# Second attention of a two-layer block: steps of two key blocks, scores in all of PSUM, weighted sums added in SBUF

## The chip, the cores and the metric

The kernel runs on one core of a Trainium2 chip. A core has a matrix engine (TensorE, PE in the profile; its weight loads are PEld), VectorE (DVE), ScalarE (ACT), GpSimd (POOL) and SyncE (SP), which issues most DMAs. Engines run their own instruction queues in order and wait for each other by semaphores. TensorE writes into PSUM, which has 8 banks of 128 x 512 fp32; VectorE and ScalarE read it. Everything here is fp32, and each fp32 matmul of the program appears as two matmuls in the profile, so a "round" below is one pass of 512 columns through the array. The array can be split into tiles that work side by side: four tiles of 64x64, eight of 32x64 (32 rows of contraction, 64 output rows), four of 128x32. The profile writes this shape in each group.

The metric is the time of one execution on the device, in microseconds; less is better.

## The reference

Input x has 16 images of 256 channels and 32x32 = 1024 positions. Layer 0 is an attention with 4 heads of 64; layer 1 is group norm, an attention with 8 heads of 32, group norm and an mlp of 1024 hidden channels.

```
x = res0 @ w_out + b_out + xs                       # layer 0, attention with 4 heads of 64
x = x + attention(group_norm(x, gn1), qkv_w, proj_w, proj_b, phys_bias)   # 8 heads of 32
h = gelu(mlp_w1 @ group_norm(x, gn2) + mlp_b1)
return x + mlp_w2 @ h + mlp_b2
```

In each attention, `softmax(q k^T / sqrt(d)) v`; the bias `phys_bias` is one number per head.

## The kernel before

All 16 images are run by one loop over `b`. For each image: the first attention (`attention_a`), the mlp's hidden half of the image before (`hidden`), the projections of the second attention (`qkv_1`), the second attention (`attention_b`), and then the next image. Work that has no place of its own on TensorE, "pieces", is laid between the steps of the second attention: the projections of its own second channel half (`own`, 7 pieces), the mlp's output half of the image before (`outputs`, 16 half reduces, from `mlp`), and the first attention's projections for the next image (`first`, 12). Image 0 has only its own 7, because it has no predecessor and its `first` pieces ran earlier; image 15 has its own 7 and 8 half reduces, the others being left for the end. Order is written out by hand: the program order of the pieces, and `Later`, a list of functions that run after so many steps (`tick`).

Softmax is done without subtracting a maximum: scores are transposed (keys on partitions), exp goes over them, the weighted sum is a matmul with v, and the sum over keys is made by adding the exps of the 8 key blocks on VectorE (`es`) and one matmul with ones (`den`) per item.

The second attention has 4 items per image: query half t (512 queries) by channel half c (4 heads). One step is one key block of 128 keys: `scores` (L410) makes 4 heads x 128 x 512 scores in four PSUM banks (two `wide` tiles of two banks), ScalarE's exp (L422) reads each wide tile into an `e` tile in SBUF; then `weigh` (L431) multiplies the exps of the step before with v, adding up over all 8 key blocks in one PSUM bank, `acc`. VectorE adds the exps (L448). At the end of an item ScalarE copies `acc` to SBUF (L455), `normalise` makes the denominator (L463) and `denominators` sends it through a small DMA (spread), a reciprocal (L267), a row in DRAM and a broadcast DMA (`rd`) back, after which `scale` (L478) multiplies. When both channel halves of a query half are done, `project` runs the output projection (`j`, through `product`, L246, and L509).

PSUM before: three `wide` tiles of two banks, taken in turn (the one used longest ago is next), and two single banks, used in turn for `acc` and `den`. Scores take two wide tiles a step; a filler takes one. The half reduces of the mlp keep their wide tile (`kept`) over two pieces. With `cols[0]` at 32 the fillers run as 128x32 tiles, the shape of `weigh`, so within a step the array changes shape from 128x32 to 32x64 and back.

`run` calls one step, then `tick`, then the fillers of that step. `gn_g`, from which the own pieces are made, shares its buffer (tag `res`) with the result of query half 0.

Of the kernel before, what the change touches and what calls it, by code (L numbers as in the profile page):

```python
# [8 lines left out]
F32 = mybir.dt.float32  # L9
# [5 lines left out]
P = 128  # L15
# [173 lines left out]
def first_pass(ctx, tc, x, out, k):  # L189
# [10 lines left out]
        tc.tile_pool(name="ps_s", bufs=1, space=bass.MemoryType.PSUM)  # L200
    )
    ps_a = ctx.enter_context(
        tc.tile_pool(name="ps_a", bufs=2, space=bass.MemoryType.PSUM)
    )

    dram = ctx.enter_context(
# [7 lines left out]
    def use(n):  # L214
        order.remove(n)
        order.append(n)
# [4 lines left out]
        use(n)  # L221
        return ps_s.tile([P, 2, TB], F32, tag=f"s{n}", name=name)

    def bank(name):
        return ps_a.tile([P, TB], F32, tag="acc", name=name)


    dsum, isum = (act.tile([P, 4 * TB // P], F32, name=n) for n in ("dsum", "isum"))
# [60 lines left out]
    def attention_a(b, qT, kT, v, project):  # L289
# [24 lines left out]
        def weigh(i, kb, e):  # L314
            t, c = items[i]
            if kb == 0:
                if i % 2:
                    acc = wide(f"acc_{key}_{i}", 2)
                    accs[i] = [acc[:, h, :] for h in range(2)]
                else:  # L320
                    accs[i] = [bank(f"acc_{key}_{i}_{h}") for h in range(2)]
# [12 lines left out]
            if kb == 1:  # L334
                sums[i] = work.tile([P, 2, TB], F32, tag="es", name=f"es_{key}_{i}", bufs=4)
            nc.vector.tensor_add(sums[i], held[i] if kb == 1 else sums[i], e)  # L336
            if kb == SB - 1:
                r = res[:, c, t * TB : (t + 1) * TB]
                one, two = accs.pop(i)
                nc.scalar.copy(r, one)  # L340
                nc.vector.tensor_add(r, r, two)
# [52 lines left out]

    def attention_b(b, qT, kT, v, project):
        key, D = f"b_{b}", D1
        G = P // D
        items = [(t, c) for c in range(CC) for t in range(NT)]  # L400
        units = [(i, kb) for i in range(len(items)) for kb in range(SB)]
        res = {}
        accs, held, sums = {}, {}, {}

        def scores(i, kb):
            t, c = items[i]
            tiles = [wide(f"s_{key}_{i}_{kb}_{n}") for n in range(G // 2)]
            for g in range(G):
                for h in range(0, P, HALF):
                    nc.tensor.matmul(  # L410
                        tiles[g // 2][h : h + HALF, g % 2, :],
                        kT[g * D : (g + 1) * D, c, kb * P + h : kb * P + h + HALF],
                        qT[g * D : (g + 1) * D, c, t * TB : (t + 1) * TB],
                        start=True,
                        stop=True,
                    )
            es = []
            for n, s in enumerate(tiles):
                e = work.tile(
                    [P, 2, TB], F32, tag="e", name=f"e_{key}_{i}_{kb}_{n}", bufs=8  # L420
                )
                nc.scalar.activation(e, s, AF.Exp, scale=float(D) ** -0.5)  # L422
                es.append(e)
            return i, kb, es

        def weigh(i, kb, es):
            t, c = items[i]
            if kb == 0:
                accs[i] = bank(f"acc_{key}_{i}")
            for g in range(G):  # L430
                nc.tensor.matmul(  # L431
                    accs[i][g * D : (g + 1) * D, :],
                    v[:, kb, c * G + g],
                    es[g // 2][:, g % 2, :],
                    start=(kb == 0),
                    stop=(kb == SB - 1),
                )
            if kb == 0:
                held[i] = es
                return  # L440
            if kb == 1:
# [4 lines left out]
            for n, e in enumerate(es):  # L446
                d = sums[i][n]
                nc.vector.tensor_add(d, held[i][n] if kb == 1 else d, e)  # L448
            if kb == SB - 1:
                if t not in res:  # L450
                    res[t] = act.tile(
                        [P, CC, TB], F32, tag="res1" if t else "res", name=f"res_{key}_{t}"
                    )
                r = res[t][:, c, :]
                nc.scalar.copy(r, accs.pop(i))  # L455
                last = i == len(items) - 1
                later.after(1 if last else 2, lambda: normalise(i, r, last))

        def normalise(i, r, last):
            t, c = items[i]  # L460
            den = bank(f"den_{key}_{i}")
            for g in range(G):
                nc.tensor.matmul(  # L463
                    den[g * D : (g + 1) * D, :],
                    k["eones"][:, c * G + g],
                    sums[i][g // 2][:, g % 2, :],
                    start=True,
                    stop=True,
                )
            denominators(  # L470
                f"{key}_{i}", den_copy(f"{key}_{i}", den), TB,
                ((3, 5) if b + 1 < B else (1, 1)) if last else (1, 3),
                lambda full: scale(i, r, last, full),
            )

        def scale(i, r, last, full):
            t, c = items[i]
            tc.keep_in_program_order(nc.vector.tensor_mul(r, r, full))  # L478
            if c == CC - 1:
                wait = (10 if b + 1 < B else 1) if last else 1  # L480
                later.after(wait, lambda: project(t, res[t]))

        cols[0] = D
        pending = None
        for u in units:
            now = scores(*u)
            if pending:
                weigh(*pending)
            pending = now
            yield  # L490
        weigh(*pending)
        yield
        cols[0] = P
# [183 lines left out]


    def mlp(b, xb, hn):
        gs, held, slot = {}, [], []  # L680

        def hidden(t, hc):
            ps = wide(f"m1_{b}_{t}_{hc}")[:, 0, :]
# [9 lines left out]
            nc.scalar.activation(g, ps, AF.Gelu, bias=k["m1b"][:, hc : hc + 1])  # L693
            gs[t, hc] = g


        def reduce(t, co, half, part):
            n = TB // 2
            if part == 0:
                held.append(wide(f"m2_{b}_{t}_{co}_{half}")[:, 0, :n])  # L700
                kept.add(order[-1])
                slot.append(order[-1])
            else:
                use(slot[-1])
                kept.discard(slot.pop())
            ps = held[-1]
            for hc in range(part * HC // 2, (part + 1) * HC // 2):
                product(
                    ps,
                    k["w2"][:, hc, co * P : (co + 1) * P],  # L710
                    gs[t, hc][:, half * n : (half + 1) * n],
                    start=(hc == 0),
                    stop=(hc == HC - 1),
                )
            if part == 0:
                return
# [4 lines left out]
            if half:  # L721
# [5 lines left out]
        return (  # L727
            [lambda t=t, hc=hc: hidden(t, hc) for t in range(NT) for hc in range(HC)],
            [
                lambda t=t, co=co, half=half, part=part: reduce(t, co, half, part)  # L730
                for t in range(NT) for co in range(CC) for half in range(2)
                for part in range(2)
            ],
        )

# [38 lines left out]

    later.after(2, fold_bias)
    hidden, outputs = [], []
    last = NT * CC * SB - 1
    for b in range(B):
        if b + 1 < B:
            xs[b + 1] = load_x(b + 1)  # L780
# [18 lines left out]

        run_pieces(qk[:n] + v[:1])  # L800
        own = [v[1], qk[n], v[2], qk[n + 1], v[3], *qk[n + 2 :]]
        fill = {m: [piece] for m, piece in enumerate(own)}
        rest = outputs + (first if b > 0 else [])
        end = []
        if b == B - 1:

            rest, end = rest[:8], rest[8:]
        for m, piece in enumerate(rest):
            at = len(own) + m * (last + 1 - len(own)) // max(1, len(rest) - 1)
            fill.setdefault(at, []).append(piece)  # L810
        hn = []
        run(
            attention_1(
# [21 lines left out]
    row = bank("ok_row")  # L835
# [290 lines left out]
```

## Time and profile before

| | us |
|---|---|
| runs | 3879.7, 3879.98, 3877.6 (median 3879.7) |
| profiled execution | 3877.58 |
| its span, first to last instruction | 3875.7 |
| TensorE busy | 3846.9 (99%) |
| VectorE busy | 2116.0 (55%) |
| ScalarE busy | 2048.2 (53%) |
| granted TensorE clock, mean | 1.000 |

Group rows read: line, engine, operation, output and inputs, shape, count; busy us in all and mean ns of one; then the idle time of the engine ahead of them and what ended it. Timeline rows read: start (us), length (us), engine, line, operation, and how many instructions were merged. Matmuls are pipelined and overlap, so the length of a TensorE group is more than what it adds; the distance from one group's start to the next is its cost. The first attention, the hidden half and the projections are not touched by the change; the second attention of images 1 to 14 lasts 131.6 us in the image shown in the prediction (1286.9 to 1418.6).

### The profile page before, as it was taken

The numbers are of one execution on the slowest core, as the hardware profiler recorded it, in microseconds if no ns is written. First come the engines' busy times: TensorE is split into PE (matmuls) and PEld (weight loads), VectorE is DVE, ScalarE is ACT, GpSimd is POOL, SyncE is SP. The second block draws the span as 40 slices with busy tenths as digits, with TensorE's granted clock in tenths as the row PEclk, the third lists the DMA queues.
The fourth block names the chain that finished last, engine by engine and source line by source line (L and its number), as shares of the span: only waits on it lengthen the run. The fifth ranks groups of instructions, "written<-read, shape, count | busy, mean of one in ns | idle before, by whom it ended". The sixth has DMA issues, their size and how long they took to land.

```text
span 3875.7 us, 86863 instructions
## 1 busy us (share of the span) xinstructions
PE 3846.9 (99%) x38637; PEld 1435.3 (37%) x38637; DVE 2116.0 (55%) x2569; ACT 2048.2 (53%) x2369; POOL 84.8 (2%) x252
## 2 busy tenths in 40 slices
PE   9999999999999999999999999999999999999999
PEld 3333343333433334333343333333333333333335
DVE  4574545645456455555545556455464555645562
ACT  4654645546455554545545555454554545545461
POOL 1000000000000000000000000000000000000000
PEclk9999999999999999999999999999999999999999
DMA  2000000000000000000000000010000000000000
GB/s 83 12 13 15 27 12 32 13 12 27 12 32 15 10 27 12 32 15 13 29 7 32 15 16 26 7 32 15 16 26 7 32 15 18 24 10 19 14 13 23
DMA packets 62445, 78.54 MB, mean 20 GB/s; under 512 B 35344, under 2 KB 36880, under 8 KB 62064
## 3 DMA queue, kind: packets, MB, share of 16 engines
q1 hardware_dynamic: 57728, 68.72, 5.8%
q8 instruction: 304, 4.98, 0.5%
q10 hardware_dynamic: 3712, 3.80, 0.3%
q14 instruction: 77, 0.63, 0.1%
q0 software_dynamic: 624, 0.41, 0.1%
HBM read 54.54 MB, written 17.56 MB: 19 GB/s over the span
## 4 chain that ended last, share of the span: by engine, by line
PE 92%; DVE 5%; ACT 1%; issue 1%; DMA 0%; POOL 0%; ACTq 0%; SPq 0%; DVEq 0%
PE s_b L410 14%; PE acc_b L431 13%; PE m L685 12%; PE m L246 11%; PE s_a L303 10%; PE acc_a L324 9%; PE qk_b L246 6%; PE qk_a L246 6%; PE v_b L246 3%; PE v_a L246 3%; PE j L246 3%; DVE es_a L336 2%; PE o L246 2%; PE den_b L463 1%; ACT e_a L311 1%
## 5 line engine op out<-in xcount | busy, mean ns | idle before, releaser
L422 ACT ACTIVATE e_b<-s_b 128x1024 f32<-128x1024 f32 x1024 | 994.3, 1023 | 601.4 <-PE s_b L410 596.3
L448 DVE TENSOR_TENSOR es_b<-es_b,e_b 128x1024 f32<-128x1024 f32 x768 | 905.0, 1221 | 436.1 <-ACT e_b L422 436.1
L311 ACT ACTIVATE e_a<-s_a 128x1024 f32<-128x1024 f32 x512 | 520.9, 1024 | 450.6 <-PE s_a L303 437.1
L410 PE MATMUL s_b<-q,k 32*64 32x512 f32 x8192 | 581.4, 613 | 1.2 <-DVE x L509 0.6
L303 PE MATMUL s_a<-q,k 64*64 64x512 f32 x4096 | 562.1, 593 | 2.4 <-DVE x L509 2.4
L324 PE MATMUL acc_a<-e_a,v 64*64 64x512 f32 x4096 | 555.1, 589 | 0.0
L431 PE MATMUL acc_b<-e_b,v 128*32 128x512 f32 x4096 | 546.2, 604 | 0.1
L336 DVE TENSOR_TENSOR es_a<-es_a,e_a 128x1024 f32<-128x1024 f32 x384 | 468.9, 1221 | 111.8 <-ACT e_a L311 107.0
L246 PE MATMUL m<-g,w 128*32 128x256 f32 (+1 forms) x7616 | 482.7, 379 | 0.3 <-DVE mean_h L545 0.3
L685 PE MATMUL m<-gn_h,w 128*128 128x512 f32 x1024 | 458.2, 599 | 3.8 <-DVE mean_g L545 3.8
L246 PEld LDWEIGHTS m<-g,w 128*32 128x32 f32 (+1 forms) x7616 | 279.4, 112 | 253.4 <-issue 101.3
L693 ACT ACTIVATE g<-m,m1b 128x512 f32<-128x512 f32 x256 | 174.2, 687 | 341.4 <-PE m L685 341.2
L448 DVE TENSOR_TENSOR es_b<-e_b,e_b 128x1024 f32<-128x1024 f32 x128 | 151.1, 1222 | 246.8 <-ACT e_b L422 246.8
L324 PEld LDWEIGHTS acc_a<-e_a,v 64*64 64x64 f32 x4096 | 183.2, 133 | 260.9 <-issue 233.0
L685 PEld LDWEIGHTS m<-gn_h,w 128*128 128x128 f32 x1024 | 188.5, 190 | 241.3 <-issue 226.9
L303 PEld LDWEIGHTS s_a<-q,k 64*64 64x64 f32 x4096 | 167.3, 133 | 280.6 <-issue 207.2
L246 PE MATMUL qk_a<-x,wp 128*32 128x512 f32 (+1 forms) x1856 | 244.2, 594 | 7.8 <-DMA wp<-in_L_conv_w_proj_dram 6.0
L410 PEld LDWEIGHTS s_b<-q,k 32*64 32x64 f32 x8192 | 126.0, 129 | 307.8 <-ACT e_b L422 133.6
L246 PE MATMUL qk_b<-gn_g,wq 128*32 128x512 f32 (+1 forms) x1280 | 234.1, 592 | 0.0
L431 PEld LDWEIGHTS acc_b<-e_b,v 128*32 128x32 f32 x4096 | 82.3, 108 | 407.5 <-issue 403.1
L615 DVE TENSOR_TENSOR v<-v_b,eones 128x512 f32<-128x512 f32 x64 | 44.0, 688 | 263.8 <-PE v_b L246 263.8
L246 PEld LDWEIGHTS qk_b<-gn_g,wq 128*32 128x32 f32 (+1 forms) x1280 | 81.9, 126 | 137.4 <-issue 127.8
(111 smaller groups left out, 1986.1 us busy)
## 6 DMA issues: line engine op xcount, KB each, us to landing
x<-in_x_dram SPq DMA_DIRECT2D x32, 512.0 KB, 4.4
rd_a<-row_a SPq DMA_DIRECT2D x64, 256.0 KB, 3.9
rd_b<-row_b SPq DMA_DIRECT2D x256, 64.0 KB, 2.0
out_dram<-x SPq DMA_DIRECT2D x64, 256.0 KB, 2.0
w<-in_L_conv_mlp_w_dram ACTq DMA_DIRECT2D x2, 1024.0 KB, 16.1
sp_b<-d_b SPq DMA_DIRECT2D x64, 8.0 KB
row_b<-inv_b SPq DMA_DIRECT2D x64, 8.0 KB, 1.4
wq<-in_L_conv_qkv_w_dram ACTq DMA_DIRECT2D x1, 768.0 KB, 11.9
```

The lines of the kernel that those rows point to most:

```text
L246: nc.tensor.matmul(o[sl], w[:, sl], r, **flags)
L303: nc.tensor.matmul(s[h : h + HALF, g, :], kT[g * D : (g + 1) * D, c, kb * P + h : kb * P + h + HALF], qT[g * D : (g + 1) * D, c, t * TB : ...
L311: nc.scalar.activation(e, s, AF.Exp, scale=float(D) ** -0.5)
L324: nc.tensor.matmul(accs[i][h][g * D : (g + 1) * D, :], v[h * HALF : (h + 1) * HALF, kb, c * 2 + g], e[h * HALF : (h + 1) * HALF, g, :], st ...
L336: nc.vector.tensor_add(sums[i], held[i] if kb == 1 else sums[i], e)
L410: nc.tensor.matmul(tiles[g // 2][h : h + HALF, g % 2, :], kT[g * D : (g + 1) * D, c, kb * P + h : kb * P + h + HALF], qT[g * D : (g + 1) * ...
L422: nc.scalar.activation(e, s, AF.Exp, scale=float(D) ** -0.5)
L431: nc.tensor.matmul(accs[i][g * D : (g + 1) * D, :], v[:, kb, c * G + g], es[g // 2][:, g % 2, :], start=(kb == 0), stop=(kb == SB - 1),)
L448: nc.vector.tensor_add(d, held[i][n] if kb == 1 else d, e)
L615: nc.vector.tensor_mul(d, ps, v_scale.unsqueeze(1).to_broadcast([P, 2, C // D, D]))
L685: nc.tensor.matmul(ps, k["w1"][:, cc, hc * P : (hc + 1) * P], hn[0][:, cc, t * TB : (t + 1) * TB], start=(cc == 0), stop=(cc == CC - 1),)
L693: nc.scalar.activation(g, ps, AF.Gelu, bias=k["m1b"][:, hc : hc + 1])
```

## The change

One step of the second attention takes two key blocks. Their scores fill all 8 banks: the first block's heads 0 and 1 go into the two single banks (`b0`, `b1`), heads 2 and 3 into a wide tile, the second block's into two wide tiles. The exp of heads 0 and 1 of the first block becomes two instructions of 512 columns. Since no bank is left for an accumulator that lives over an item, `weigh` adds up only the two blocks of a step, in `b0`, and the sum goes to SBUF: by a ScalarE copy in an item's first step, by a VectorE add `res += acc` in the three others. `den` takes `b1`. The exp sums are added in two parts, ahead of and behind `weigh`, in that program order. The items run as (1,0), (0,0), (0,1), (1,1) instead of (0,0), (1,0), (0,1), (1,1) (query half, channel half), so that the partial sums of the first item are not written into the buffer that the own pieces still read. Fillers are laid two old pieces to a step: the mlp's reduces become whole (8 instead of 16 halves, no tile kept over two pieces), `first` goes in groups of two or three, with one piece beside the last own piece and one after the last step. The scale of an item follows one step after its reciprocal (of the new, double steps) instead of three.

```diff
-        tc.tile_pool(name="ps_a", bufs=2, space=bass.MemoryType.PSUM)
+        tc.tile_pool(name="ps_a", bufs=1, space=bass.MemoryType.PSUM)
...
-    def bank(name):
-        return ps_a.tile([P, TB], F32, tag="acc", name=name)
+    def bank(name, n):
+        return ps_a.tile([P, TB], F32, tag=f"b{n}", name=name)
...
     def attention_b(b, qT, kT, v, project):
-        items = [(t, c) for c in range(CC) for t in range(NT)]
-        units = [(i, kb) for i in range(len(items)) for kb in range(SB)]
+        items = [(NT - 1, 0)]
+        items += [(t, 0) for t in range(NT - 1)] + [(t, 1) for t in range(NT)]
+        units = [(i, kb) for i in range(len(items)) for kb in range(0, SB, 2)]
...
-            tiles = [wide(f"s_{key}_{i}_{kb}_{n}") for n in range(G // 2)]
+            for m in range(2):
+                if m == 0:
+                    one, two = (bank(f"s_{key}_{i}_{kb}_{n}", n) for n in range(2))
+                    tiles = [None, wide(f"s_{key}_{i}_{kb}_1")]
+                    outs = [one, two, tiles[1][:, 0, :], tiles[1][:, 1, :]]
+                else:
+                    tiles = [wide(f"s_{key}_{i}_{kb + 1}_{n}") for n in range(2)]
+                    outs = [tiles[g // 2][:, g % 2, :] for g in range(G)]
+                for g in range(G):
+                    for h in range(0, P, HALF):
+                        k0 = (kb + m) * P + h
+                        nc.tensor.matmul(
+                            outs[g][h : h + HALF, :],
...
+                    for to, s in (
+                        [(e, tiles[n])] if tiles[n] is not None
+                        else [(e[:, 0, :], one), (e[:, 1, :], two)]
+                    ):
+                        nc.scalar.activation(to, s, AF.Exp, scale=float(D) ** -0.5)
...
+        def add(i, kb, es, block):
...
+            for n in range(G // 2):
                 d = sums[i][n]
-                nc.vector.tensor_add(d, held[i][n] if kb == 1 else d, e)
+                ins = nc.vector.tensor_add(d, es[n] if kb == 0 else d, es[2 * block + n])
+                if block:
+                    tc.keep_in_program_order(ins)
...
+        def weigh(i, kb, es):
+            t, c = items[i]
+            acc = bank(f"acc_{key}_{i}_{kb}", 0)
+            for m in range(2):
+                for g in range(G):
+                    nc.tensor.matmul(
+                        acc[g * D : (g + 1) * D, :],
+                        v[:, kb + m, c * G + g],
+                        es[2 * m + g // 2][:, g % 2, :],
+                        start=(m == 0),
+                        stop=(m == 1),
+                    )
...
+            if kb == 0:
+                nc.scalar.copy(r, acc)
+            else:
+                nc.vector.tensor_add(r, r, acc)
+            if kb == SB - 2:
+                later.after(1, lambda: normalise(i, r, i == len(items) - 1))
...
-            den = bank(f"den_{key}_{i}")
+            den = bank(f"den_{key}_{i}", 1)
...
-                ((3, 5) if b + 1 < B else (1, 1)) if last else (1, 3),
+                ((3, 5) if b + 1 < B else (1, 1)) if last else (1, 1),
...
             now = scores(*u)
+            add(*now, 0)
             if pending:
                 weigh(*pending)
+            add(*now, 1)
...
-        def reduce(t, co, half, part):
+        def reduce(t, co, half):
-            if part == 0:
-                held.append(wide(f"m2_{b}_{t}_{co}_{half}")[:, 0, :n])
-                kept.add(order[-1])
-                slot.append(order[-1])
-            else:
-                use(slot[-1])
-                kept.discard(slot.pop())
-            for hc in range(part * HC // 2, (part + 1) * HC // 2):
+            ps = wide(f"m2_{b}_{t}_{co}_{half}")[:, 0, :n]
+            for hc in range(HC):
...
-    last = NT * CC * SB - 1
+    last = NT * CC * SB // 2 - 1
...
-        fill = {m: [piece] for m, piece in enumerate(own)}
-        rest = outputs + (first if b > 0 else [])
+        fill = {m: own[2 * m : 2 * m + 2] for m in range((len(own) + 1) // 2)}
+        now, end = outputs, []
+        if b == 0:
+            first = []
         if b == B - 1:
-            rest, end = rest[:8], rest[8:]
-        for m, piece in enumerate(rest):
-            at = len(own) + m * (last + 1 - len(own)) // max(1, len(rest) - 1)
-            fill.setdefault(at, []).append(piece)
+            now, end = outputs[:4], outputs[4:]
+        rest = [[piece] for piece in now]
+        at = len(fill)
+        if first:
+            fill[at - 1] = fill[at - 1] + first[:1]
+            fill[last + 1] = first[-1:]
+            pairs = [first[1:4], first[4:7], first[7:9], first[9:-1]]
+            for m, pair in enumerate(pairs):
+                rest.insert(3 * m + 2, pair)
+        for m, pieces in enumerate(rest):
+            fill[at + m] = pieces
```

More of the change, by code (lines that the diff above doesn't have):

```diff
@@ L320, in weigh @@
                 else:
-                    accs[i] = [bank(f"acc_{key}_{i}_{h}") for h in range(2)]
+                    accs[i] = [bank(f"acc_{key}_{i}_{h}", h) for h in range(2)]
             for h in range(2):
@@ L399, in attention_b @@
         G = P // D
-        items = [(t, c) for c in range(CC) for t in range(NT)]
-        units = [(i, kb) for i in range(len(items)) for kb in range(SB)]
-        res = {}
-        accs, held, sums = {}, {}, {}
+        items = [(NT - 1, 0)]
+        items += [(t, 0) for t in range(NT - 1)] + [(t, 1) for t in range(NT)]
+        units = [(i, kb) for i in range(len(items)) for kb in range(0, SB, 2)]
+        res, sums = {}, {}
         def scores(i, kb):
             t, c = items[i]
-            tiles = [wide(f"s_{key}_{i}_{kb}_{n}") for n in range(G // 2)]
[L408 to L415, printed above, removed]
-                    )
[L417 to L423, printed above, removed]
-            return i, kb, es
@@ L426, in weigh @@
[L426 to L441, printed above, removed]
+            es = []
@@ new lines, in scores @@
+            for m in range(2):
[11 more added lines that the diff above has]
+                            outs[g][h : h + HALF, :],
+                            kT[g * D : (g + 1) * D, c, k0 : k0 + HALF],
+                            qT[g * D : (g + 1) * D, c, t * TB : (t + 1) * TB],
+                            start=True,
+                            stop=True,
+                        )
+                for n in range(G // 2):
+                    e = work.tile(
+                        [P, 2, TB], F32, tag="e", name=f"e_{key}_{i}_{kb + m}_{n}", bufs=8
+                    )
+                    for to, s in (
[3 more added lines that the diff above has]
+                        nc.scalar.activation(to, s, AF.Exp, scale=float(D) ** -0.5)
+                    es.append(e)
@@ L442, in weigh @@
+            return i, kb, es
+        def add(i, kb, es, block):
+            if kb == 0 and block == 0:
                 sums[i] = [
@@ L445, in weigh @@
                 ]
-            for n, e in enumerate(es):
+                return
+            for n in range(G // 2):
                 d = sums[i][n]
[L448 to L452, printed above, removed]
-                    )
[L454 to L457, printed above, removed]
+                ins = nc.vector.tensor_add(d, es[n] if kb == 0 else d, es[2 * block + n])
[12 more added lines that the diff above has]
+                        stop=(m == 1),
+                    )
+            if t not in res:
+                res[t] = act.tile(
+                    [P, CC, TB], F32, tag="res1" if t == NT - 1 else "res",
+                    name=f"res_{key}_{t}",
+                )
+            r = res[t][:, c, :]
+            if kb == 0:
[4 more added lines that the diff above has]
+                later.after(1, lambda: normalise(i, r, i == len(items) - 1))
         def normalise(i, r, last):
             t, c = items[i]
-            den = bank(f"den_{key}_{i}")
+            den = bank(f"den_{key}_{i}", 1)
             for g in range(G):
@@ L679, in mlp @@
     def mlp(b, xb, hn):
-        gs, held, slot = {}, [], []
+        gs = {}
         def hidden(t, hc):
@@ L694, in hidden @@
             gs[t, hc] = g
-        def reduce(t, co, half, part):
+        def reduce(t, co, half):
             n = TB // 2
-            if part == 0:
-                held.append(wide(f"m2_{b}_{t}_{co}_{half}")[:, 0, :n])
-                kept.add(order[-1])
-                slot.append(order[-1])
-            else:
-                use(slot[-1])
-                kept.discard(slot.pop())
-            ps = held[-1]
-            for hc in range(part * HC // 2, (part + 1) * HC // 2):
+            ps = wide(f"m2_{b}_{t}_{co}_{half}")[:, 0, :n]
+            for hc in range(HC):
                 product(
@@ L714, in reduce @@
                 )
-            if part == 0:
-                return
             y = xb[:, co, t * TB + half * n : t * TB + (half + 1) * n]
@@ L729, in mlp @@
             [
-                lambda t=t, co=co, half=half, part=part: reduce(t, co, half, part)
+                lambda t=t, co=co, half=half: reduce(t, co, half)
                 for t in range(NT) for co in range(CC) for half in range(2)
-                for part in range(2)
             ],
@@ L801, in first_pass @@
         own = [v[1], qk[n], v[2], qk[n + 1], v[3], *qk[n + 2 :]]
-        fill = {m: [piece] for m, piece in enumerate(own)}
-        rest = outputs + (first if b > 0 else [])
-        end = []
+        fill = {m: own[2 * m : 2 * m + 2] for m in range((len(own) + 1) // 2)}
+        now, end = outputs, []
+        if b == 0:
+            first = []
         if b == B - 1:
-            rest, end = rest[:8], rest[8:]
-        for m, piece in enumerate(rest):
-            at = len(own) + m * (last + 1 - len(own)) // max(1, len(rest) - 1)
-            fill.setdefault(at, []).append(piece)
+            now, end = outputs[:4], outputs[4:]
[9 more added lines that the diff above has]
+            fill[at + m] = pieces
         hn = []
@@ L834, in first_pass @@
     nc.vector.tensor_mul(both, ok[:, 0:1], ok[:, 1:2])
-    row = bank("ok_row")
+    row = bank("ok_row", 0)
     nc.tensor.transpose(row[0:1, :P], both, k["ident"])
```

## The prediction

> **What bounds the kernel now.** I read the page first (engine shares, chain of waits, groups), then TensorE's waits, then timelines of the second attention in three places: image 5 (filled steps), image 0 (bare steps), and the start of the stage. The page:
>
> ```profile
> PE 3846.9 (99%) x38637; PEld 1435.3 (37%) x38637; DVE 2116.0 (55%) x2569; ACT 2048.2 (53%) x2369; POOL 84.8 (2%) x252
> PE 92%; DVE 5%; ACT 1%; issue 1%; DMA 0%; POOL 0%; ACTq 0%; SPq 0%; DVEq 0%
> L422 ACT ACTIVATE e_b<-s_b 128x1024 f32<-128x1024 f32 x1024 | 994.3, 1023 | 601.4 <-PE s_b L410 596.3
> L448 DVE TENSOR_TENSOR es_b<-es_b,e_b 128x1024 f32<-128x1024 f32 x768 | 905.0, 1221 | 436.1 <-ACT e_b L422 436.1
> ...
> L341 DVE TENSOR_TENSOR res_a<-res_a,acc_a 128x512 f32<-128x512 f32 x64 | 43.8, 684 | 15.1 <-ACT res_a L340 14.6
> L282 ACT COPY d_b<-den_b 128x512 f32<-128x512 f32 x64 | 37.6, 587 | 9.2 <-PE den_b L463 9.1
> ```
>
> TensorE is never free; VectorE and ScalarE idle almost half the time, waiting for it. Only TensorE's own time, or a wait newly put in front of it, can move the end. But its busy time hides what happens between matmul groups. TensorE's timeline in image 5 (start us, length us, group; groups overlap, so starts are compared) shows it:
>
> ```profile
> 1318.04 1.11 PE L410 MATMUL s_b<-q,k 32*64 32x512 f32 x16
> 1319.09 1.07 PE L431 MATMUL acc_b<-e_b,v 128*32 128x512 f32 x8
> 1319.97 1.91 PE L246 MATMUL m<-g,w 128*32 128x256 f32 x32
> 1321.81 1.11 PE L410 MATMUL s_b<-q,k 32*64 32x512 f32 x16
> 1322.86 1.06 PE L431 MATMUL acc_b<-e_b,v 128*32 128x512 f32 x8
> 1323.74 1.04 PE L463 MATMUL den_b<-es_b,eones 128*32 128x512 f32 x8
> 1324.60 1.91 PE L246 MATMUL m<-g,w 128*32 128x256 f32 x32
> ```
>
> A group of two rounds of 512 columns with no change of array shape takes 0.86 us (den, 1323.74 to 1324.60); in the first attention, where every group is 64x64, starts stand 0.86 apart throughout. The scores (32x64) take 1.05 to the next start, 0.19 too much; acc, the first group at 128x32, 0.88, 0.02 too much; the fill of 32 takes 1.84 to the next scores where 32 more of the same cost 1.72 (a fill of 64 runs 3.56), 0.12 too much. So each step pays 0.33 us for going to the 32x64 shape and back. The stage of image 5 (1286.9 to 1418.6, 131.6 us) is its pure work, 120.9, plus 32 x 0.33: nothing else is lost there.
>
> The helpers beside one step (T = 1330.20; the row at 1330.68 is the second score round, from a narrower window), and image 0, where most steps have no fill:
>
> ```profile
> 1330.20 1.11 PE L410 MATMUL s_b<-q,k 32*64 32x512 f32 x16
> ...
> 1330.68 0.63 PE L410 MATMUL s_b<-q,k 32*64 32x512 f32 x8
> ...
> 1331.36 1.94 ACT L422 ACTIVATE e_b<-s_b 128x1024 f32<-128x1024 f32 x2 [1.82 <-PE s_b L410]
> 1332.41 2.36 DVE L448 TENSOR_TENSOR es_b<-es_b,e_b 128x1024 f32<-128x1024 f32 x2 [1.41 <-ACT e_b L422]
> ...
> 162.84 1.11 PE L410 MATMUL s_b<-q,k 32*64 32x512 f32 x16
> 181.23 1.11 PE L410 MATMUL s_b<-q,k 32*64 32x512 f32 x16
> ```
>
> The first exp starts 1.15 after the scores; exps follow each other at 0.92 (two take 1.94, one 1.02), adds at 1.14 (2.36 less 1.22). Image 0 needs 18.39 us for an item of 8 blocks.
>
> **The change, part by part.** Terms are against the profiled execution, 3877.6 us (span 3875.7 and 1.9 around it), which lies 2.1 below the median, 3879.7.
>
> *1. Half the shape changes.* A step now takes two key blocks: four score rounds, four weigh rounds, the fill. 512 steps become 256. In the 14 images with full fill (1 to 14): 16 x 0.33 = 5.33 us each, **-74.6**. Images 0 and 15 are counted below. This holds if the second block's score rounds come at 0.43. Bounds: the first two score rounds start 0.48 apart, and if every round of this shape did, a step would give back 0.10; if the whole 0.19 belonged to each block, 0.19. I take 0, as in the 64x64 rounds, the nearest rows without a change of shape.
>
> *2. A filled step, walked through.* From T: scores to 1.90, weigh 1.90 to 3.64, fill (3.45, two old pieces) to 7.2. ScalarE: the first exp is split into two of 512 columns. No row shows one: half of 1.02 is 0.51, the longest 512 row (Gelu, 0.687) the other end; I take 0.60, near the copy's 0.587, at a pitch of 0.5 (half of 0.92 is 0.46). Starts 1.14, 1.64, then the wide ones 2.14, 3.06, 3.98, end 5.0. The weigh must wait until bank b0 is read: 1.14 + 0.60 + 0.05 (an add starts 0.03 after its exp) = 1.79, before 1.90; at Gelu's length 1.88. Nothing is lost. A filler uses the wide tile read first: free at 3.2, before 3.64. VectorE, in the built order: two adds from 2.27, the new res += acc (0.685 by the L341 row, 192 of them, 132 us in all, beside TensorE) at 4.54, two adds to 7.5, the mlp's output (0.48) from 7.4 to 7.9. Bank b0 is free at 5.2, long before the next scores at 7.2. The filler's tile is free at 7.93, and the next step writes it as its last score tile, at 7.2 + 0.91 = 8.11: 0.17 to spare. So steady steps cost nothing; this narrow margin is the cover to watch. VectorE must next start at 9.5.
>
> A rule weighs against this part. The Trainium skill, "Perfetto Trace Analysis", section "Matmuls", wants independent matmul groups to rotate through PSUM banks, so that evacuation of one overlaps the next. The change does the opposite. Were the emptying of the accumulator exposed in every step, with res += acc ending at 4.55 and TensorE ready at 3.64, it would cost 0.9 x 256 = 230 us, and the sum would come out near 4070. I follow the rows: 3.45 us of fill stand in between.
>
> *3. Division.* The waits of (1,3) steps become (1,1) double ones. Reciprocal at T+6.8; before, the last broadcast landed 5.8 us after the reciprocal (1327.37; issues to 1331.18, 2.0 to land), so T+12.6, 5.4 into the next step; the multiply is due there at 7.4. No wait. But it (0.69, pitch 0.6) stands ahead of the mlp output on VectorE: tile free at 8.53 against 8.11, a stall of 0.43 us. It meets an mlp filler in steps 10 and 14 (step 6 has qk pieces, read by ScalarE): 2 x 0.43 x 14 = **+12.0** (0 to 24).
>
> *4. The first step.* Scores fill all three wide tiles, there is nothing to weigh, and the filler wants the tile whose exp ends at 3.16: TensorE, ready at 1.9, waits 1.26. Before, a third tile was free; only 0.21 was lost (second scores 1.32 instead of 1.11). **+14.7** for 14 images (4 to 18).
>
> *5. Image 0: 12 bare steps.* No fill covers the loop now. With kb = 4 and 6, scores wait for b0: exps 1.14 to 2.24, adds to 4.54, res += acc to 5.2, next scores at 5.25 and 5.75 (behind the multiply). With kb = 2 the accumulator is copied by ScalarE after five exps: 5.0. With kb = 0 b1 waits for the denominator's copy: 5.63. Together 21.6 per item against 18.39. Whole stage: 6.8 (step 0) + 2 x 7.2 + 5.5 + 12 x 5.4 - 2 (covered by the projection) + 3.4 (projection) + 1.7 (last weigh) = 94.7 against 85.9 (130.0 to 215.9): **+8.8** (3 to 14).
>
> *6. Image 15: 8 bare steps.* 6.8 + 14.4 + 5.5 + 4 x 7.2 + 0.4 + 8 x 5.4 - 2 + 3.4 + 1.7 = 102.3 against 102.9 (3686.1 to 3789.0). Before, the half-done reduce held a wide tile, and six scores took 2.00 instead of 1.11 to 1.3; whole reduces end that: **-0.6**.
>
> *7. The rest, at nothing.* Fill, projections, mlp, qkv are the same matmuls; TensorE's order elsewhere is the same. DMAs: no count changes; an output DMA on SP waits for VectorE's mlp add at the end of a step, and what stands behind it on SP, the next spread, is due some 5 us later. POOL keeps its two small adds per item. Item order (query half 1 first) only lets res be written early, because `gn_g` shares half 0's buffer: no time by itself.
>
> Sum: -74.6 + 12.0 + 14.7 + 8.8 - 0.6 = **-39.7**: 3837.9 on the profiled basis, **3840** beside the median.
>
> **Rivals.**
>
> *A. VectorE's end of step becomes the wait (slower).* Place: the last score tile of the 112 steps of images 1 to 14 whose filler ends in the mlp add. For: margin 0.17, and 192 new VectorE reads of PSUM. Against: 56 adds of 1.14 and all else make 83 us of VectorE in a stage of 126, and each step begins with idle VectorE until 2.27. If it runs d late, it costs 112 x (d - 0.17); it decides from d = 0.52, where 39.7 are gone. With d = 0.8: +71, 3910.
>
> *B. The extra belongs to the 32x64 rounds, not to the change of shape (the change doesn't do what it says).* For: 0.48 between the first two. Against: the shortest score matmuls of this shape last 587 ns, no longer than the 64x64 ones (593 in the mean), so nothing but the first round looks stretched. 0.10 x 256: +27, 3867; with 0.19, +49, 3889.
>
> *C. The stalls don't come.* Exps a little shorter or adds more tightly packed take parts 3 and most of 4 away, and image 0 half: -26, 3814.
>
> **How the numbers follow.** My case 0.53 (3822 to 3862); C 0.17; B 0.18 (a third of it over the old time); A 0.12. The range reaches from just under C's time, 3812, to B's upper end, 3888, leaving out A and the last of C, some 2 in 10. A measurement tells 0.2% (7.8 us) from no change: under 3872 faster, 0.80; within, 0.06 (B's middle); over 3887.5, 0.14 (A, and B's upper end).
>
> **What would show it.** Right: steps of 7.2 us in images 1 to 14 with scores of 1.9; TensorE's starts after scores and fill with the same 0.33 per step; the stage near 128 us; bare steps of 5.4 in image 0; about 1.3 us before the first filler, its weight load waiting for an exp. Part 3: score groups stretched by 0.4 after the multiply, released by VectorE's mlp line. Wrong: four score rounds of 2.1 us or more (B); weigh groups waiting for the 512 exps, or score loads waiting for VectorE in most steps (A); or TensorE time moving outside the second attention, which I hold unchanged.

## The result, and where the time went

| | before | after |
|---|---|---|
| median, us | 3879.2 | 3837.0 |
| profiled execution, us | 3877.58 | 3836.97 |
| its span, us | 3875.7 | 3835.1 |

The ratio is 0.9892 [0.9875, 0.9910]; the kernel measured again beside the experiments gave 3836.78 and 0.9899 [0.9883, 0.9916]. Between the profiled executions the change is worth -40.6 us; the sum of the prediction was -39.7.

The page after, engine shares, chain of waits and the group that is new:

```profile
PE 3783.2 (99%) x38637; PEld 1508.9 (39%) x38637; DVE 2214.2 (58%) x2761; ACT 2033.7 (53%) x2625; POOL 86.1 (2%) x252
...
PE 90%; DVE 5%; issue 2%; ACT 2%; DMA 1%; POOL 0%; SPq 0%; ACTq 0%; POOLq 0%; DVEq 0%
...
L477 DVE TENSOR_TENSOR res_b<-res_b,acc_b 128x512 f32<-128x512 f32 x192 | 131.1, 683 | 190.9 <-PE acc_b L461 190.9
```

The same 38637 matmuls take 63.7 us less busy time, yet the end moves by only 40.6. The difference is new waiting on TensorE. TensorE's waits after (who waited, for whom: us in all, times, longest) have three rows that before did not:

```profile
PE v_b L246 <- ACT e_b L437: 19.2, 16, 1.2
...
PE s_b L422 <- DVE res_b L477: 4.9, 8, 0.9
...
PE s_b L422 <- ACT res_b L475: 0.9, 5, 0.2
```

The new `res += acc` costs VectorE 131.1 us in 192 instructions and brings TensorE 4.9 us of listed waits, in 8 places, all in the steps without filler (bare steps) of images 0 and 15. TensorE's timeline of image 5 shows where both signs come from:

```profile
1278.81 1.97 PE L422 MATMUL s_b<-q,k 32*64 32x512 f32 x32
1281.99 1.93 PE L246 MATMUL v_b<-wq,gn_g 128*32 128x256 f32 x32 [1.20 <-ACT e_b L437]
...
1285.57 1.97 PE L422 MATMUL s_b<-q,k 32*64 32x512 f32 x32
...
1315.30 1.97 PE L422 MATMUL s_b<-q,k 32*64 32x512 f32 x32
1317.20 1.92 PE L461 MATMUL acc_b<-e_b,v 128*32 128x512 f32 x16
1318.94 3.64 PE L246 MATMUL m<-g,w 128*32 128x256 f32 x64
1322.51 1.97 PE L422 MATMUL s_b<-q,k 32*64 32x512 f32 x32
...
1392.92 2.40 PE L422 MATMUL s_b<-q,k 32*64 32x512 f32 x32
1395.25 1.92 PE L461 MATMUL acc_b<-e_b,v 128*32 128x512 f32 x16
```

Read starts. A filled step is 1315.30 to 1322.51, 7.21 us: scores 1.90, weigh 1.74, fill 3.57. Four score rounds of 0.43 are 1.72, so they bear 0.18 too much, as two rounds did before (0.19); the weigh bears 0.02 and the fill 0.13. The 0.33 of going to the 32x64 shape and back is the same, paid once for two blocks. Against it stand the 1.20 us ahead of the first filler, and two score groups, behind steps 10 and 14, that take 2.32 to the next start (2.33 in the last rows) instead of 1.90.

By stage, from scores start to scores start: image 1 begins 5.2 us later relative to image 0; each of images 1 to 14 takes 236.72 us in place of 239.92, 3.20 less, -44.8 in all; image 15 with everything behind it is 0.5 shorter, and what is ahead of image 0's stage 0.5 shorter too. That is the whole -40.6. The last 0.5 can't be put down to the change: over the runs of this document image 0's stage begins anywhere from 129.4 to 132.2 us. In image 5 the 3.2 lie inside the second attention (132.67 to 129.48, from its first scores to the next image's first attention); nothing outside it moved.

### The profile page after: what moved, and what is told of

It is laid out like the page before. It is cut to its first block, busy times and chain, and to the rows that moved or that the text cites. A ratio compares the mean times of both kernels' runs of the same rounds, so it can differ in the third digit from the quotient of the medians.

```text
span 3835.1 us, 87391 instructions
## 1 busy us (share of the span) xinstructions
PE 3783.2 (99%) x38637; PEld 1508.9 (39%) x38637; DVE 2214.2 (58%) x2761; ACT 2033.7 (53%) x2625; POOL 86.1 (2%) x252
## 4 chain that ended last, share of the span: by engine, by line
PE 90%; DVE 5%; issue 2%; ACT 2%; DMA 1%; POOL 0%; SPq 0%; ACTq 0%; POOLq 0%; DVEq 0%
PE s_b L422 12%; PE m L709 12%; PE acc_b L461 12%; PE m L246 11%; PE s_a L303 10%; PE acc_a L324 9%; PE qk_b L246 6%; PE qk_a L246 6%; PE v_b L246 3%; PE j L246 3%; PE v_a L246 3%; DVE es_a L336 2%; PE o L246 2%; PE den_b L485 1%; ACT e_a L311 1%
## 5 line engine op out<-in xcount | busy, mean ns | idle before, releaser
L437 ACT ACTIVATE e_b<-s_b 128x1024 f32<-128x1024 f32 (+1 forms) x1280 | 982.7, 864 | 469.4 <-PE s_b L422 469.4
L422 PE MATMUL s_b<-q,k 32*64 32x512 f32 x8192 | 536.3, 601 | 5.8 <-DVE res_b L477 4.9
L461 PE MATMUL acc_b<-e_b,v 128*32 128x512 f32 x4096 | 492.1, 598 | 0.0
L246 PE MATMUL m<-g,w 128*32 128x256 f32 (+1 forms) x7616 | 464.0, 379 | 0.0
L422 PEld LDWEIGHTS s_b<-q,k 32*64 32x64 f32 x8192 | 173.8, 130 | 294.0 <-issue 155.7
L461 PEld LDWEIGHTS acc_b<-e_b,v 128*32 128x32 f32 x4096 | 108.5, 109 | 351.6 <-ACT e_b L437 194.7
L477 DVE TENSOR_TENSOR res_b<-res_b,acc_b 128x512 f32<-128x512 f32 x192 | 131.1, 683 | 190.9 <-PE acc_b L461 190.9
L246 PE MATMUL qk_a<-x,wp 128*32 128x512 f32 (+1 forms) x1856 | 234.1, 594 | 7.2 <-DMA wp<-in_L_conv_w_proj_dram 5.9
```

The lines of the kernel that those rows point to most:

```text
L246: nc.tensor.matmul(o[sl], w[:, sl], r, **flags)
L422: nc.tensor.matmul(outs[g][h : h + HALF, :], kT[g * D : (g + 1) * D, c, k0 : k0 + HALF], qT[g * D : (g + 1) * D, c, t * TB : (t + 1) * TB] ...
L437: nc.scalar.activation(to, s, AF.Exp, scale=float(D) ** -0.5)
L461: nc.tensor.matmul(acc[g * D : (g + 1) * D, :], v[:, kb + m, c * G + g], es[2 * m + g // 2][:, g % 2, :], start=(m == 0), stop=(m == 1),)
L477: nc.vector.tensor_add(r, r, acc)
```

## The experiments

The theory is the prediction's: half of the shape changes go, and waits in three places are paid for that. The rivals are B (the 0.19 belongs to the score rounds and not to the change of shape), A (VectorE's end of step sets the time, or is about to), and one more: that the regrouping of the fillers and the whole reduces is what brings the gain. Experiments 1 to 4 are one run each; the kernel before took 3877.07 beside them, and the changed kernel was not run there, so they are set against its 3837.0. The others are medians of 4 to 10 runs.

**1 and 2. A shape change put back, and its control.** Between the two blocks' scores of a step stands a matmul of 2 columns; in `e1_shape_between` it has the 128x32 shape, in `e2_same_shape_between` the 32x64 shape of the scores. The score rounds that follow overwrite what it writes. The listing shows both edits at one place; each kernel has one of them.

```diff
             for m in range(2):
...
+                if m:
+                    nc.tensor.matmul(                      # e1: 128x32
+                        outs[0][0:32, 0:2], k["eones"][:, 0], k["eones"][:, 0, 0:2],
+                        start=True, stop=True,
+                    )
+                    nc.tensor.matmul(                      # e2, in its place: 32x64
+                        outs[0][0:HALF, 0:2],
+                        kT[0:D, c, (kb + m) * P : (kb + m) * P + HALF],
+                        qT[0:D, c, t * TB : t * TB + 2],
+                        start=True, stop=True,
+                    )
                 for g in range(G):
```

> One matmul of 2 columns at the 128x32 shape is put between the two key blocks' scores in every step; what it writes is overwritten by the scores, and nothing is left out. Theory (half the changes of shape made the gain): two more changes in each of 256 steps, 0.33 us a step, so filled steps go from 7.21 to about 7.55 us, scores of four rounds from 1.90 to 2.2 or 2.3, and the time to about 3837 + 80 = 3917 us (less in the 20 bare steps, where TensorE has time to spare), near the kernel before. Rival (the gain came from longer runs or fewer waits, and the array's shape is no matter): no more than its control e2, 3840 to 3850.

> The control of e1: a matmul of 2 columns at the 32x64 shape of the scores in the same place, overwritten by them too. Theory: it costs only itself, 0.01 to 0.06 us a step, 3840 to 3853 us, and the score group stays under 2.0 us. Rival (any interruption of the score run costs as much as a change of shape): as e1, about 3917.

Measured: 3900.25 and 3848.48. TensorE's timeline of a filled step of image 5 in the first,

```profile
1335.78 1.11 PE L427 MATMUL s_b<-q,k 32*64 32x512 f32 x16
1336.83 0.22 PE L420 MATMUL s_b<-eones 128*32 128x2 f32 x2
1336.98 1.11 PE L427 MATMUL s_b<-q,k 32*64 32x512 f32 x16
1338.02 1.92 PE L466 MATMUL acc_b<-e_b,v 128*32 128x512 f32 x16
1339.76 3.64 PE L246 MATMUL m<-g,w 128*32 128x256 f32 x64
1343.33 1.11 PE L427 MATMUL s_b<-q,k 32*64 32x512 f32 x16
```

and, of the second, the starts of two steps:

```profile
1320.51 1.11 PE L428 MATMUL s_b<-q,k 32*64 32x512 f32 x16
...
1327.79 1.11 PE L428 MATMUL s_b<-q,k 32*64 32x512 f32 x16
```

The step takes 7.55 us with the change of shape (1335.78 to 1343.33) and 7.28 without (1320.51 to 1327.79; steps of this kind take 7.26 to 7.29 all through that run), against 7.21. So the small matmul costs some 0.07 in the shape of the scores, and the change of shape there and back 0.27 more; by the prediction's rows it was 0.33 in all. In the first, each block's scores alone take 1.05 again, as before the change. B falls.

In all, the first adds 63.2 us to the 3837.0 where some 80 were expected. The trace shows why it is less. The stage of each of images 1 to 14 grows by 4.17 us, 14 x 4.17 = 58 of the 63. Fifteen filled steps would give 15 x 0.34 = 5.1. The first step stays at 6.76, because the 1.20 wait shrinks to 0.9 in exchange. The two stretched score groups are gone (2 x 0.43 = 0.86), because the last score tile is wanted later, and so is a small stretch of 0.07 behind step 2: 5.1 - 0.86 - 0.07 = 4.17. A delay on TensorE pays for the waits that it covers, which the expectation had left out.

**3. VectorE's order at the end of a step.** `e6_sum_first` puts `weigh` and its sum ahead of all four exp adds, in program order, so that the sum is the first thing VectorE does in a step and the adds and the mlp's output come later.

```diff
             now = scores(*u)
-            add(*now, 0)
             if pending:
                 weigh(*pending)
+            add(*now, 0)
             add(*now, 1)
...
-                if block:
-                    tc.keep_in_program_order(ins)
+                tc.keep_in_program_order(ins)
...
-                nc.vector.tensor_add(r, r, acc)
+                tc.keep_in_program_order(nc.vector.tensor_add(r, r, acc))
```

> res += acc is put ahead of all four exp adds on VectorE, in program order. Theory (VectorE's end of step has only some 0.2 us to spare against the last score tile): VectorE waits for the weigh until T+3.87, its adds end at about 9.1 instead of 7.5, and the mlp's output frees its tile at 9.55 (10.15 behind the multiply) against 8.11. Steps 7 and 11 lose about 1.4 us, 10 and 14 about 2.0 (0.43 now): +6 us per image in images 1 to 14, +3 in image 15, together about 3925 us, in score groups stretched to 3.3 to 3.9 us and released by the mlp add. Bare steps get shorter by up to 0.5 us in two of four. Rival (VectorE is only 58% busy, so its order is no matter): 3832 to 3840.

Measured: 3971.24, 134 us slower than the change as it is, more than expected. TensorE in image 5, with an mlp filler and the multiply in front:

```profile
1405.28 1.95 PE L422 MATMUL s_b<-q,k 32*64 32x512 f32 x24
1408.31 1.09 PE L422 MATMUL s_b<-q,k 32*64 32x512 f32 x8 [1.09 <-DVE x L731]
1409.33 1.92 PE L460 MATMUL acc_b<-e_b,v 128*32 128x512 f32 x16
```

and VectorE beside it:

```profile
1402.03 0.69 DVE L476 TENSOR_TENSOR res_b<-res_b,acc_b 128x512 f32<-128x512 f32 x1 [5.84 <-PE acc_b L460]
1402.64 4.62 DVE L452 TENSOR_TENSOR es_b<-es_b,e_b 128x1024 f32<-128x1024 f32 x4
...
1407.78 0.48 DVE L731 SCALAR_TENSOR_TENSOR x<-m,m2b,x 128x256 f32<-128x256 f32 x1
```

VectorE stood idle for 5.84 us until the weigh was done, then did its whole step in a row, and the last 8 of the 32 score matmuls wait for the mlp's output at the end of it. Scores take 4.05 with the multiply in front (1405.28 to 1409.33) and 3.38 in the next step, without it, near the 3.3 to 3.9 that were expected. What was not foreseen is the same wait after step 2, where VectorE's read of a v projection ends late: TensorE's waits have it as a row of its own.

```profile
PE s_b L422 <- DVE x L731: 43.6, 58, 1.1
PE s_b L422 <- DVE v L638: 24.5, 16, 1.5
```

So the mechanism of A is there, at the place that it named. In the changed kernel it takes no time from a usual filled step, because the built order, two adds ahead of the sum, fills the time in which VectorE would wait.

**4. The regrouped fillers alone.** `e7_fill_pairs_only` is the kernel before, one key block to a step, with whole reduces and two fillers on every second step.

```diff
-        fill = {m: own[2 * m : 2 * m + 2] for m in range((len(own) + 1) // 2)}
+        fill = {2 * m: own[2 * m : 2 * m + 2] for m in range((len(own) + 1) // 2)}
...
-            fill[at - 1] = fill[at - 1] + first[:1]
+            fill[2 * at - 2] = fill[2 * at - 2] + first[:1]
...
-            fill[at + m] = pieces
+            fill[2 * (at + m)] = pieces
```

(against the changed kernel; scores, weigh, banks and item order are those of before)

> The kernel before with one part of the change alone: whole mlp reduces, and fillers laid two old pieces to every second step, in the new order; steps stay at one key block and accumulators in PSUM. Theory (the gain is in the halved changes of shape): every step still pays 0.33 us, and a bare step ahead of a filled one makes the filled one's scores wait about 0.16 us for an exp; image 15 gains 5 us, since no tile is held over two pieces. 3875 to 3910 us. Rival (regrouping the fillers made the gain): about 3840.

Measured: 3922.76, 45.7 slower than before, and worse than the worst expected. Two steps on TensorE in image 5:

```profile
1329.56 1.11 PE L410 MATMUL s_b<-q,k 32*64 32x512 f32 x16
...
1331.60 1.28 PE L410 MATMUL s_b<-q,k 32*64 32x512 f32 x16
1332.81 1.06 PE L431 MATMUL acc_b<-e_b,v 128*32 128x512 f32 x8
...
1337.26 1.11 PE L410 MATMUL s_b<-q,k 32*64 32x512 f32 x16
```

There are still two shape changes in the pair, so it can at best take the 2 x 3.77 = 7.54 of before. It takes 7.70: the scores behind a step without fill take 1.21 instead of 1.05. The image period is 3.2 us longer in all but two images. In image 5 twelve score groups are stretched like this, eight to 1.21 and four to 1.27, 2.2 in all. Another 1.2 is lost at the end: from the projection `j` to the next image's first attention it is 13.72 us instead of 12.48, and there the last weigh waits for exps. Image 15 with what stands behind it became 2.3 us shorter, where 5 were expected from the reduce that keeps no tile over two pieces. The regrouping by itself is a loss, so the gain is not from it.

**5. The multiply behind the mlp's output.** `e3_scale_behind` issues the division's multiply of a middle item after the step's fillers, so that the mlp's add comes first on VectorE.

```diff
-    later = Later()
+    later, behind = Later(), []
...
-            later.after(waits[1], lambda: then(full))
+            if len(waits) == 3:
+                later.after(waits[1], lambda: behind.append(lambda: then(full)))
+            else:
+                later.after(waits[1], lambda: then(full))
...
-                ((3, 5) if b + 1 < B else (1, 1)) if last else (1, 1),
+                ((3, 5) if b + 1 < B else (1, 1)) if last else (1, 1, 1),
...
+            while behind:
+                behind.pop(0)()
```

> The multiply by the reciprocal goes behind the step's fillers in program order, so that the mlp's output comes first on VectorE. Theory: the stall of 0.43 us after steps 10 and 14 goes (score groups of 2.32 become 1.90), in images 1 to 14 and once in image 15: 29 x 0.43 = 12.5 us less than the changed kernel, about 3825. Rival (the stretched groups wait for something else, an exp or the next bank): 3837, with the groups still at 2.3.

Measured: 3825.98, ratio to the kernel before 0.9867 [0.9851, 0.9884]; 10.8 below the changed kernel's 3836.78, measured beside it. The score group that took 2.32 is back at 1.90, and image 5's stage is 0.85 shorter, both stalls:

```profile
1361.02 1.97 PE L425 MATMUL s_b<-q,k 32*64 32x512 f32 x32
1362.92 1.92 PE L464 MATMUL acc_b<-e_b,v 128*32 128x512 f32 x16
```

**6. A filler inside the first step.** The first step's wait was to go by putting the v piece that stands behind its scores between the two blocks. `e4_filler_between` calls it when the second block's tiles have been taken.

```diff
                     tiles = [wide(f"s_{key}_{i}_{kb + 1}_{n}") for n in range(2)]
                     outs = [tiles[g // 2][:, g % 2, :] for g in range(G)]
+                if m and middle:
+                    middle.pop()()
...
-                        nc.tensor.matmul(
+                        ins = nc.tensor.matmul(
...
+                        if ordered:                        # i == 0 and kb <= 2
+                            tc.keep_in_program_order(ins)
...
-        own = [v[1], qk[n], v[2], qk[n + 1], v[3], *qk[n + 2 :]]
-        fill = {m: own[2 * m : 2 * m + 2] for m in range((len(own) + 1) // 2)}
+        own = [qk[n], v[2], qk[n + 1], v[3], *qk[n + 2 :]]
+        fill = {m: own[max(0, 2 * m - 1) : 2 * m + 1] for m in range(len(own) // 2 + 1)}
```

> In the first step only, the second v piece is put between the two key blocks' scores, at the price of two more changes of shape. Theory (the first filler waits 1.2 us for a wide tile): the step falls from 6.76 to about 6.1 us, because the wait of 1.2 goes, 0.33 and a wait of some 0.3 for the first block's wide tile come: 16 x 0.65 = 10 us less than the changed kernel, about 3827. Rival (what waits is the start of the exps, which the table load and the stage's start set): the wait comes back in the next filler or in the second step's scores, 3835 to 3842.

> Both edits, of e3 and e4. Theory: they lie in different steps and add up, 22 us less than the changed kernel, about 3815, 0.983 of before. Rival: they share a cause, and the sum stays under 15 us.

Measured: `e4_filler_between` 3879.15, 1.0004 [0.9994, 1.0014], and with the edit of experiment 5 added (`e8_both`) 3874.34, 0.9991 [0.9981, 1.0000]: 42 and 38 us slower than the changed kernel. Both expectations missed. The start of image 5's stage in the first:

```profile
1296.24 1.11 PE L425 MATMUL s_b<-q,k 32*64 32x512 f32 x16
1299.41 2.37 PE L246 MATMUL v_b<-wq,gn_g 128*32 128x256 f32 x32 [2.06 <-ACT e_b L442]
...
1304.84 1.92 PE L246 MATMUL qk_b<-gn_g,wq 128*32 128x512 f32 x16 [1.12 <-ACT e_b L442]
1306.70 1.97 PE L425 MATMUL s_b<-q,k 32*64 32x512 f32 x32
```

The step takes 10.46 us here instead of 6.76; in nine of images 1 to 14 it takes 9.1. The wide tiles are handed out in turn. The first block has one, and the second block's two were already taken, so the filler got the first block's again and stood behind its exp, with the second block's scores behind the filler. This was an error of the edit: the idea was not tested by it.

**7. The same with a free tile.** In `e9_filler_free_tile` the two added lines stand ahead of the second block's tiles; `e10_both_free_tile` adds experiment 5.

```diff
             for m in range(2):
+                if m and middle:
+                    middle.pop()()
                 if m == 0:
...
-                if m and middle:
-                    middle.pop()()
                 for g in range(G):
```

> As e4, but the filler between the two blocks of the first step is given its tile before the second block's scores are given theirs, so it gets a wide tile that nothing occupies. Theory (in e4 the filler waited for the first block's own tile until the exp at T+3.17, and the next filler for the second block's): scores 0 to 0.9, filler 1.05 to 2.8, second block from 2.9 with its second half at 3.2, next filler 4.2 to 6.0; the step is 6.1 to 6.2 us instead of 6.76, 16 x 0.6 = 10 us less than the changed kernel, about 3827. Rival (two more changes of shape and the exps' later start eat it): 3834 to 3842.

> The edits of e3 and e9 together. Theory: they lie in different steps and add up: 10.8 us (measured for e3) and 10, about 3816 us, 0.984 of before. Rival: no more than e3 alone, 3826.

Measured: 3827.99, 0.9871 [0.9856, 0.9886], and 3813.25, 0.9832 [0.9819, 0.9846]. The second is faster than both kernels, 23.5 us below the changed one. By image the two gains add up: a period is 0.85 shorter with experiment 5, 0.71 with `e9_filler_free_tile` and 1.56 with both. TensorE's timeline of the first at the same place:

```profile
1277.49 1.11 PE L425 MATMUL s_b<-q,k 32*64 32x512 f32 x16
...
1280.40 1.35 PE L425 MATMUL s_b<-q,k 32*64 32x512 f32 x16
1281.68 1.93 PE L246 MATMUL qk_b<-gn_g,wq 128*32 128x512 f32 x16
1283.54 1.97 PE L425 MATMUL s_b<-q,k 32*64 32x512 f32 x32
```

The step is 6.05 us instead of 6.76. Of the 1.20 of waiting, 0.23 come back in the second block's scores (1.28 instead of 1.05: its second tile is now the first block's again), and a second change of shape is paid. 0.71 x 14 = 9.9, beside 8.8 measured (on another chip than the 3836.78; the kernel before took 3877.65 and 3877.97 on the two).

## Why the prediction was right, by its steps

*Part 1, half the shape changes: right.* Rows show 1.90, 1.74 and 3.57 for the three groups of a step, and experiment 1 pays the change of shape again, step by step, where the control does not. The page "TensorEngine Tiling (Array Packing)" of the Trainium skill, section "Key Properties", says that a change of tiling mode drains TensorE, without a price. The runs show that a change costs time, there and back about 0.3 us; that it is a drain, no run here shows.

*Part 2, the filled step: right, by a small margin.* A filled step takes 7.20 or 7.21 where 7.2 was worked out, and longer only by what else it holds (`den`, a third piece). In the rows of part 3 below, the mlp's output ends 8.47 after the step's start, and the multiply ahead of it is 0.60 of that, so 7.87 without it, where 7.93 was worked out. The stall there is 0.43; if it is as long as the output is late, the tile is wanted at 8.04 and not at 8.11, and the margin is the 0.17 that was forecast. The 512-column exps, for which before had no row, take 594 ns against the 0.60 taken; ScalarE's groups, kept apart by shape:

```profile
L437 ACT ACTIVATE e_b<-s_b 128x512 f32<-128x512 f32 x512 | 278.4, 594 | 469.4 <-PE s_b L422 469.4
```

The rule that was weighed, to rotate matmul groups through PSUM banks (the Trainium skill, "Perfetto Trace Analysis", section "Matmuls"), would have made about 4070 of it, had the emptying been exposed in every step. In images 1 to 14 neither a weigh nor a score load waits for the sum that is read from `b0`; all 23 waits of scores and their weight loads for it (`res_b`, L477) lie in images 0 and 15. In their bare steps, where no other matmuls stand between, the rule holds: an item of image 0 takes 21.48 us there against 18.39 before. So in this kernel what decides is how much other work TensorE has while the bank is emptied.

*Part 3, the two stalls of 0.43: right.* VectorE of image 5 after, in the second of them, and the weight load of the last 8 score matmuls that it releases:

```profile
1390.82 2.35 DVE L452 TENSOR_TENSOR es_b<-es_b,e_b 128x1024 f32<-128x1024 f32 x2
1393.10 0.69 DVE L500 TENSOR_TENSOR res_b<-res_b,rd_b 128x512 f32<-128x512 f32 x1
1393.70 0.48 DVE L732 SCALAR_TENSOR_TENSOR x<-m,m2b,x 128x256 f32<-128x256 f32 x1
```

```profile
1394.23 0.21 PEld L422 LDWEIGHTS s_b<-q,k 32*64 32x64 f32 x8 [0.24 <-DVE x L732]
```

The step began at 1385.71: the adds end at 7.46, the mlp's output at 8.47, where 7.5 and 8.53 had been worked out. Taking the multiply away from there gave 10.8 back, of the 12.0 forecast (0.85 an image, 11.9, by the periods). One more such stall, of 0.43, stands in image 15 (3695.25 to 3697.57), which the sum did not count.

*Part 4, the first step: right.* TensorE waits 1.20 us, taken as 1.26, 16 times (19.2 in all); the step takes 6.76, taken as 6.8. Experiment 7 took 8.8 of it back, net of a shape change.

*Part 5, image 0: the mechanism right, the size not.* The bare steps came as walked through. TensorE's timeline of one item there (in brackets the wait that ended; the item begins at 160.85, and each row is what is left of a step's scores once `b0` or `b1` is free):

```profile
166.70 1.97 PE L422 MATMUL s_b<-q,k 32*64 32x512 f32 x30 [0.18 <-ACT res_b L475]
...
171.95 1.97 PE L422 MATMUL s_b<-q,k 32*64 32x512 f32 x30 [0.43 <-DVE res_b L477]
...
177.69 1.97 PE L422 MATMUL s_b<-q,k 32*64 32x512 f32 x30 [0.92 <-DVE res_b L477]
...
182.33 2.82 PE L422 MATMUL s_b<-q,k 32*64 32x512 f32 x32
```

The rows with a VectorE wait stand 5.25 and 5.74 behind the row ahead of them, where 5.25 and 5.75 had been worked out. An item is 160.85 to 182.33, 21.48 us, taken as 21.6, and the stage up to the last `den` 94.2 (129.51 to 223.69), taken as 94.7. Yet image 0 lost 5.2 and not 8.8. The term that was mis-sized is the 85.9 of before: it ended that stage at the last weigh. Behind that start, TensorE of before waited for the last exps and adds:

```profile
214.14 3.15 PE L431 MATMUL acc_b<-e_b,v 128*32 128x512 f32 x16
217.83 2.19 PE L463 MATMUL den_b<-es_b,eones 128*32 128x512 f32 x8 [0.54 <-DVE es_b L448]
219.95 2.81 PE L303 MATMUL s_a<-q,k 64*64 64x512 f32 x24
```

From the last weigh's start to the first attention it is 5.81 us there, of which 1.74 are two blocks' weigh; after, the last double weigh starts at 221.97 and the first attention at 224.66, 2.69. These 3.1 us were a gain that the sum left out.

*Part 6, image 15: the number right, by luck*, -0.5 against -0.6. Its stage up to the end of the last weigh takes 102.83 us in both kernels (3686.13 to 3788.96 before, 3646.06 to 3748.89 after), where 102.3 was worked out; 0.43 of the difference is the stall of part 3 in this image. The 0.5 that was gained lies behind the stage; why, I did not find.

*Part 7:* nothing moved outside the stage, as said. That the order of the items costs nothing by itself was only argued: the old order was not tried, since with it the first partial sum would go into the buffer that the own pieces still read.

*Images 1 to 14 as a whole:* -3.20 each, where parts 1, 3 and 4 make -3.42 (47.9 in all, measured 44.8). 0.07 of the missing 0.22 lie in the score group at 1299.97, 1.97 to the next start instead of 1.90, behind VectorE's read of a v projection; the rest I did not find. This loss and the gain that part 5 left out nearly cancel, so the sum came nearer to the measurement than its terms did.

*Rivals.* B fell by the rows and by experiments 1 and 2 (its lower price, 0.10 x 256, is 25.6 and not 27). A did not come, and experiment 3 shows what it costs when VectorE's order is turned. C, stalls that don't come, was wrong: they came in their places, and had to be taken away by experiments 5 and 7.

## What to carry to other kernels

Where TensorE is full, read what a pattern costs from start to start, against a stretch of the same matmuls without that pattern: 0.33 us a step in no list of waits was worth more than every wait in the list. When buffers become so few that each has one use at a time, walk through one step with every engine's order written out, ask at each tile who reads it last, and keep the steps with something extra (first, division, bare) as terms of their own. End a stage in the forecast at the same event before and after, the next stage's first instruction, or a wait between the two is lost.

## What was not expected of the hardware

- A change of array shape there and back with a 2-column matmul in it costs 0.34 us a step, a matmul of 2 columns in the shape already set 0.07.
- TensorE's list of waits does not show a short wait that falls on a weight load within a group: the two stalls of 0.43 us an image are seen as groups of length 2.40 instead of 1.97, and count as busy. The wait of 1.20 us ahead of a whole group is listed.
- A delay put on TensorE (experiment 1) gave 0.93 us an image back by ending stalls for which it left time.
